# A four-layer attention network on one core: a looser test ahead of layer 0, a new hand-over at the ends of its attention blocks, and layer 1's norms off GpSimd

## The chip, the cores and the metric

The kernel runs on one core of a Trainium2 chip. TensorE (PE) multiplies matrices into PSUM, VectorE (DVE), ScalarE (ACT) and GpSimd (POOL) work element by element, and SyncE (SP) and ScalarE issue DMA transfers. Each engine takes its instructions in the order in which they were written to its own queue, and waits on semaphores for the others. The metric is the device time of one launch in microseconds (us): 5060.61 us before, the median of three runs (5054.19 to 5061.7). All data are float32.

## The reference, cut to what matters

The input x has shape (2, 64, 64, 128): two images of 4096 tokens with 128 channels. Four layers follow one another, each added to x. The change touches the first two:

```
# layer 0: x = x + conv_attention(group_norm(x))
qkv    = xn @ w_qkv                          # 128 -> 3 x 128, 4 heads of 32
scores = q @ k.T * 32**-0.5 + pos            # pos: relative position tables, by row and by column
x      = x + softmax(scores) @ v             # over all 4096 tokens of the image

# layer 1: x = x + triangle(group_norm(x))
xn  = layer_norm(group_norm(x))
l,r = gated projections of xn                # products with sigmoid gates
out = einsum('bkjd,bkid->bijd', l, r) / 64
x   = x + (layer_norm(out) * gate) @ Wo + bo
```

Layers 2 and 3 are attention with a mixture of experts each; nothing of them is changed.

## The kernel before

`layers` runs the four layers in sequence. x stays in SBUF as 64 tiles of 128 tokens.

**The test ahead of layer 0** (`layer0`). A softmax may leave out the subtraction of the row maximum if no score can become too large, and then exponentials of scores and of position terms can be multiplied as separate factors. The kernel tests this on the data. For each image it transposes x in eight groups of 512 tokens (`group_block`, L110 on PE, statistics L113 on VectorE, copy L115 on ScalarE), makes the group norm's mean and root from them (`group_stats`), normalises the transposed image in one VectorE instruction (L289), and then, for each group and for queries and keys, projects 512 tokens (L296), squares the result on ScalarE (L304) and sums the squares of each head by four products with a 128x4 matrix of ones (L306). `tops` takes the maxima. The flag is compared with a limit on VectorE (L244), and every engine loads it and branches: to `l0_bounded`, which is the path taken with these inputs, or to the exact `l0_any`.

**Layer 0's attention** (`l0_bounded`). Eight units (image, pair of heads, half of the queries) of four blocks of 512 queries. A block goes through 32 steps k, one for each 128 keys: a score product into PSUM (L538, four 64x64-tiled matmuls for two heads), the exponential on ScalarE (L546), the multiplication by the exponentials of the column positions on VectorE (L547), and, two steps later, the value product, which adds up in the PSUM tile l0o over the whole block (`values`, L494). l0o holds two partial sums, from the first and the second 64 keys of each step, in its two banks; there is one such tile. At the end of a block its two partial sums are added for each head into the SBUF tile l0os: ScalarE copies the first (L504), VectorE adds the second (L505). `l0_finish` then transposes l0os, divides by the row sums and adds to x. Such follow-up work, and the preparation of the next unit (`l0_prepare`), is cut into pieces that are placed between the steps, one after every second step. The first image's layer-1 norms are among these pieces.

**Layer 1's start** (`layer1`, `l1_rows`). For the second image nothing of layer 0 is left to hide behind. The group norm in token order is a subtraction and a multiplication (`group_norm`, L156 and L157) for each of eight groups of 512 columns, six on VectorE and two on GpSimd; then token statistics on VectorE (L164, L165), a reciprocal root (`rstd`, L93 to L102), the normalisation on VectorE (L168) and ScalarE (L379), transposes (L394) and the gate product (L847), before the projections begin (L875). The addition of the bias bo to x, 16 operations (L924), runs on GpSimd.

The order of the instructions on each queue is fixed when the program is built; a scheduler places the instructions of concurrent strands.

Of the kernel before, what the change touches and what calls it, by code (L numbers as in the profile page):

```python
# [8 lines left out]
F32 = mybir.dt.float32  # L9
AF = mybir.ActivationFunctionType  # L10
# [29 lines left out]
class Net:  # L40
# [111 lines left out]
    def group_norm(self, eng, y, b, g, gb):  # L152

        n0 = b * NC + 4 * g
        row = [gb[:, i * C : (i + 1) * C].unsqueeze(1).broadcast_to([P, 4, C]) for i in range(2)]
        eng.tensor_tensor(y, self.x[:, n0 : n0 + 4, :], row[0], ALU.subtract)  # L156
        eng.tensor_tensor(y, y, row[1], ALU.mult)  # L157
# [95 lines left out]
    def layer0(self, xT, gst, na, nb):  # L253
# [3 lines left out]
        with ExitStack() as st:  # L257
            wp = st.enter_context(tc.tile_pool(reuse_waits="tile", name="l0w", bufs=1))
            w = self.load(wp, "wqkv", [P, 3 * C], ins["L0_conv_w_qkv"])

            pe = wp.tile([P, 2, 2 * S - 1], F32, tag="pe", name="l0pe")
            with (
# [5 lines left out]
                for i, n in enumerate("hw"):  # L268
                    nc.sync.dma_start(out=raw[: 2 * S - 1, i, :], in_=ins[f"L0_conv_pos_emb_{n}"])
# [8 lines left out]

                head = ap.tile([P, NH], F32, tag="head", name="l0head")
                nc.vector.tensor_reduce(  # L280
                    head, self.ident.rearrange("p (h d) -> p h d", d=HD), AX.X, ALU.add
                )

                norms = ps.tile([P, 2, B * NC, NH], F32, tag="norms", name="l0norms", bufs=1)
                for b in range(B):
                    for g in range(NC // 4):
                        self.group_block(ps, gst[:, b], b, g, xT[:, b, :])
                    gm, gr = self.group_stats(ps, gst[:, b], b)
                    nc.vector.tensor_scalar(  # L289
                        xT[:, b, :], xT[:, b, :], gm, gr, ALU.subtract, ALU.mult  # L290
                    )
                    for g in range(NC // 4):
                        cols = slice(g * 512, (g + 1) * 512)
                        for j in range(2):
                            pq = ps.tile([P, 512], F32, tag="misc", name=f"l0n{b}_{g}_{j}")
                            nc.tensor.matmul(  # L296
                                pq,
                                lhsT=w[:, j * C : (j + 1) * C],
                                rhs=xT[:, b, cols],
                                start=True,  # L300
                                stop=True,
                            )
                            sq = ap.tile([P, 512], F32, tag="sq", name=f"l0sq{b}_{g}_{j}")
                            nc.scalar.activation(sq, pq, AF.Square)  # L304
                            for i in range(4):
                                nc.tensor.matmul(  # L306
                                    norms[:, j, b * NC + 4 * g + i, :],
                                    lhsT=sq[:, i * P : (i + 1) * P],
                                    rhs=head,
                                    start=True,  # L310
                                    stop=True,
                                )


                top = self.tops(
                    ps,
                    "l0",
                    [
                        norms[:, 0, :, :].rearrange("p n h -> p (n h)"),
                        norms[:, 1, :, :].rearrange("p n h -> p (n h)"),  # L320
                        posn[:, 0:1],
                        posn[:, 1:2],
                    ],
                )
                s1 = self.small.tile([1, 1], F32, tag="bs1", name="l0s1")
                nc.vector.tensor_tensor(s1, top[:, 2:3], top[:, 3:4], ALU.add)
                nc.vector.tensor_scalar(s1, s1, 4.0, None, ALU.mult)
                s2 = self.small.tile([1, 1], F32, tag="bs2", name="l0s2")
                nc.vector.tensor_scalar(s2, top[:, 1:2], 2.0 / HD, None, ALU.mult)
                nc.vector.tensor_tensor(s1, s1, s2, ALU.add)  # L330
                nc.vector.tensor_tensor(s1, s1, top[:, 0:1], ALU.mult)
                small = self.at_most("l0", s1, 60.0**2)
# [24 lines left out]
    def l1_rows(self, ps, xT, b, st, gb, gpsimd=()):  # L357
# [7 lines left out]
        for g in range(NC // 4):  # L365
            blk = slice(4 * g, 4 * g + 4)
            self.group_norm(nc.gpsimd if g in gpsimd else nc.vector, y[:, blk, :], b, g, gb)
            yield
# [46 lines left out]
    def l0_bounded(self, xT, w, pe, gst, na, nb):  # L415
# [15 lines left out]
        with (  # L431
# [28 lines left out]
            os = wp.tile([P, 512], F32, tag="os", name="l0os")  # L460
# [25 lines left out]
            def values():  # L486
                unit, qb, k, es, o = waiting.pop(0)
# [13 lines left out]
                if k == NC - 1:  # L501
                    for h in range(2):
                        rows = slice(64 * h, 64 * h + HD + 1)
                        nc.scalar.copy(os[rows], o[rows, 0, :])  # L504
                        nc.vector.tensor_tensor(os[rows], o[rows, 1, :], os[rows], ALU.add)  # L505
# [15 lines left out]
            for i, unit in enumerate(units):  # L521
# [6 lines left out]
                for qb in range(4):  # L528
                    qs = slice(qb * 512, (qb + 1) * 512)
                    t = f"{b}_{pair}_{half}_{qb}"  # L530
                    o = None
                    for k in range(NC):
# [17 lines left out]
                        if o is None:  # L550
                            o = ps.tile([P, 2, 512], F32, tag="o", name=f"l0o{t}", bufs=1)
                        waiting.append((unit, qb, k, es, o))
# [98 lines left out]
    def l0_finish(self, ap, ps, unit, qb, os):  # L651
# [4 lines left out]
        yield  # L656
        po = ps.tile([P, 4, 2, 64], F32, tag="misc", name=f"l0po{t}")
        for i in range(4):
            nc.tensor.transpose(
                po[:, i, :, :].rearrange("p h d -> p (h d)"),  # L660
                os[:, i * P : (i + 1) * P],
# [129 lines left out]
    def layer1(self, xT, gst, na, nb, xp, kp):  # L791
# [5 lines left out]
        with ExitStack() as st:  # L797
# [44 lines left out]
            with tc.tile_pool(reuse_waits="tile", name="l1p", bufs=6, space=PSUM) as ps:  # L842
# [11 lines left out]
                rows = self.l1_rows(ps, xT[:, 1, :], 1, gst[:, 1], gb, gpsimd=(6, 7))  # L854
# [44 lines left out]
            with (  # L899
# [4 lines left out]
                for d8 in range(C // 8):  # L904
# [19 lines left out]
                    nc.gpsimd.tensor_tensor(  # L924
# [1236 lines left out]
```

## Time and profile before

| stretch (us) | what | PE busy | clock |
|---|---|---|---|
| 0 to 20 | x is loaded (4 MB) | 0.37 us | - |
| 20.5 to 160 | the test ahead of layer 0 | nearly all of it | 0.50 in most |
| 161 to 206 | preparing the first unit of layer 0 | 0.5 to 0.9 of it | 0.50 to 0.88 |
| 206 to 2320 | layer 0's attention | 2032.7 of 2114 us | 0.99 |
| 2320 to 2385 | layer 1's norms of the second image | 12.9, 1.6 and 10.6 of 20 us each to 2380 | 0.67, 0.50, 0.84 |
| after | rest of layer 1, layers 2 and 3 | - | mostly 1.00 |

PE is busy when a matmul is in it, whatever the clock; "clock" is the share of full speed that the throttle granted. In the listings that follow, a line of the timeline gives the start and the length in us, engine, source line, operation, output and input, the number of instructions merged, and in brackets how long the engine had been idle before and what ended the idleness. A group's line gives the number of instructions, their busy time in us with the mean in ns, and the idle time of the engine just before them with what ended most of it.

### The profile page before, as it was taken

The numbers are of one execution on the slowest core, as the hardware profiler recorded it, in microseconds if no ns is written. First come the engines' busy times: TensorE is split into PE (matmuls) and PEld (weight loads), VectorE is DVE, ScalarE is ACT, GpSimd is POOL, SyncE is SP. The second block draws the span as 40 slices with busy tenths as digits, with TensorE's granted clock in tenths as the row PEclk, the third lists the DMA queues.
The fourth block names the chain that finished last, engine by engine and source line by source line (L and its number), as shares of the span: only waits on it lengthen the run. The fifth ranks groups of instructions, "written<-read, shape, count | busy, mean of one in ns | idle before, by whom it ended". The sixth has DMA issues, their size and how long they took to land.

```text
span 5051.3 us, 79049 instructions
## 1 busy us (share of the span) xinstructions
PE 4668.8 (92%) x33638; PEld 1858.9 (37%) x33638; DVE 2942.8 (58%) x4829; ACT 2696.5 (53%) x3158; POOL 943.6 (19%) x850
## 2 busy tenths in 40 slices
PE   7999999999899999996779999999986999999999
PEld 5533333333333333333522223222334444444443
DVE  1366676767676667776665666555553544454447
ACT  2465555555555555555566766767650433333335
POOL 0100000000000000003445555555540000000008
PEclk6799999999999999998898999999997999999999
DMA  1000000000000000000000000000007000000001
GB/s 36 9 10 1 10 1 10 1 10 1 10 1 10 1 11 1 1 2 7 22 1 1 1 1 1 1 1 1 1 12 258 5 1 0 0 1 0 1 0 35
DMA packets 43359, 60.35 MB, mean 12 GB/s; under 512 B 4497, under 2 KB 25201, under 8 KB 41841
## 3 DMA queue, kind: packets, MB, share of 16 engines
q1 hardware_dynamic: 42096, 54.57, 3.5%
q8 instruction: 268, 4.39, 0.4%
q14 instruction: 99, 0.80, 0.1%
q10 hardware_dynamic: 896, 0.59, 0.0%
HBM read 42.57 MB, written 4.19 MB: 9 GB/s over the span
## 4 chain that ended last, share of the span: by engine, by line
PE 38%; DVE 5%; ACT 3%; POOL 2%; DMA 1%; issue 1%; SPq 0%; DVEq 0%; POOLq 0%; ACTq 0%
PE scl L1998 9%; PE oTl L1958 9%; PE l2sc L1372 5%; PE l2pos L1130 5%; PE l2av L1418 3%; PE f3ex L2092 2%; DVE l2es L1392 2%; POOL l2es L1395 2%; ACT l2es L1403 1%; DMA f2w<-in_L_ffn_weight_dram 1%; ACT l2es L1383 1%; PE l2po L1338 1%; DVE l2a L168 0%; PE l2pu L1130 0%; PE f3fpb L1888 0%
## 5 line engine op out<-in xcount | busy, mean ns | idle before, releaser
L547 DVE TENSOR_TENSOR l0es<-l0es,l0ew 128x1024 f32<-128x1024 f32 x1024 | 1254.6, 1229 | 619.4 <-ACT l0es L546 619.2
L546 ACT ACTIVATE l0es<-l0sc 128x1024 f32<-128x1024 f32 x1024 | 1042.2, 1023 | 701.3 <-PE l0sc L538 699.1
L494 PE MATMUL l0o<-l0es,l0v 64*33 64x512 f32 x8192 | 1093.5, 592 | 65.2 <-DVE l0os L505 59.9
L538 PE MATMUL l0sc<-l0qa,ka 64*64 64x512 f32 x8192 | 1108.9, 596 | 6.6 <-ACT l0es L546 6.6
L1403 ACT ACTIVATE l2es<-l2es 128x1024 f32<-128x1024 f32 (+3 forms) x576 | 559.5, 984 | 271.5 <-POOL l2es L1395 263.6
L1395 POOL TENSOR_TENSOR l2es<-l2es 128x1024 f32<-128x1024 f32 (+3 forms) x352 | 580.9, 1660 | 489.6 <-DVE l2es L1392 433.1
L1966 DVE TENSOR_TENSOR accl<-accl,esl 128x1024 f32<-128x1024 f32 x240 | 293.8, 1224 | 430.4 <-ACT esl L2009 426.5
L1392 DVE TENSOR_SCALAR l2es<-l2sc 128x1024 f32<-128x1024 f32 (+3 forms) x320 | 338.8, 1059 | 316.0 <-PE l2sc L1372 314.8
L494 PEld LDWEIGHTS l0o<-l0es,l0v 64*33 64x33 f32 x8192 | 263.3, 108 | 691.6 <-issue 578.9
L538 PEld LDWEIGHTS l0sc<-l0qa,ka 64*64 64x64 f32 x8192 | 301.9, 133 | 548.4 <-issue 469.7
L2009 ACT ACTIVATE esl<-scl 128x1024 f32<-128x1024 f32 x240 | 245.6, 1023 | 472.9 <-PE scl L1998 446.9
L1998 PE MATMUL scl<-l3qT,l3kT 128*128 128x512 f32 x1024 | 486.3, 595 | 0.0
L1372 PE MATMUL l2sc<-l2q,kept 32*128 32x512 f32 (+3 forms) x2304 | 390.4, 625 | 83.4 <-ACT l2es L1383 63.9
L1958 PE MATMUL oTl<-esl,l3v 128*128 128x512 f32 x960 | 451.0, 592 | 0.0
L672 POOL TENSOR_TENSOR x<-x,l0y 128x256 f32<-128x256 f32 x32 | 23.3, 728 | 2115.3 <-DVE l0y L667 1990.0
L1418 PE MATMUL l2av<-l2es,kept 128*32 128x512 f32 (+3 forms) x2304 | 315.2, 595 | 0.0
L1130 PE MATMUL l2pos<-kept 128*32 128x512 f32 x2416 | 296.9, 599 | 0.0
L1958 PEld LDWEIGHTS oTl<-esl,l3v 128*128 128x128 f32 x960 | 182.1, 190 | 225.4 <-issue 222.1
L1998 PEld LDWEIGHTS scl<-l3qT,l3kT 128*128 128x128 f32 x1024 | 187.2, 191 | 199.6 <-issue 185.7
L1383 ACT ACTIVATE l2es<-l2sc 128x1024 f32<-128x1024 f32 x224 | 226.2, 1010 | 49.7 <-PE l2sc L1372 48.6
L1372 PEld LDWEIGHTS l2sc<-l2q,kept 32*128 32x128 f32 x2304 | 116.7, 188 | 327.0 <-ACT l2es L1383 164.5
L1929 POOL TENSOR_TENSOR bothl<-accl 128x512 f32<-128x512 f32 x16 | 20.2, 1264 | 799.2 <-DVE accl L1966 799.2
(712 smaller groups left out, 4101.2 us busy)
## 6 DMA issues: line engine op xcount, KB each, us to landing
f2w<-in_L_ffn_weight_dram SPq DMA_DIRECT2D x32, 1024.0 KB, 13.1
l0ew<-l0ew SPq DMA_DIRECT2D x16, 512.0 KB, 5.2
x<-in_x_dram SPq DMA_DIRECT2D x8, 512.0 KB, 7.3
out_dram<-x SPq DMA_DIRECT2D x16, 256.0 KB, 2.3
kept<-in_L_attn_pos_rev_dram SPq DMA_DIRECT2D x1, 1792.0 KB
ew<-in_L_ffn_expert_w_dram SPq DMA_DIRECT2D x1, 512.0 KB, 4.2
kept<-in_L_attn_pos_rev_dram SPq DMA_DIRECT2D x1, 256.0 KB, 3.0
f2b<-in_L_ffn_weight_dram ACTq DMA_DIRECT2D x2, 128.0 KB, 2.8
```

The lines of the kernel that those rows point to most:

```text
L494: nc.tensor.matmul(o[64 * h : 64 * h + HD + 1, r, :], lhsT=v1[rows, k, 2 * pair + h, :], rhs=es[rows, h, :], start=(k == 0), stop=(k == NC ...
L538: nc.tensor.matmul(sc[64 * c : 64 * c + 64, h, :], lhsT=ka[rows, k0 : k0 + 64], rhs=qa[rows, k // (NC // 2), qs], start=True, stop=True,)
L546: nc.scalar.activation(es, sc, AF.Exp)
L547: nc.vector.tensor_tensor(es, es, ew[:, :, qs], ALU.mult)
L1130: nc.tensor.matmul(out[part], lhsT=lhsT[:, part], rhs=rhs, start=start, stop=stop)
L1372: nc.tensor.matmul(sc[:, h2, off:], lhsT=kT[hs, k * P : (k + 1) * P], rhs=q[hs, off:], start=True, stop=True,)
L1392: nc.vector.tensor_scalar(es[:, :, lo:], sc[:, :, lo:], root, None, ALU.mult)
L1395: nc.gpsimd.tensor_tensor(part, part, part, ALU.mult)
L1403: nc.scalar.activation(es[:, :, off:], es[:, :, off:], AF.Silu)
L1418: nc.tensor.matmul(avs[i][hs, off:], lhsT=v[:, k, hs], rhs=es[h // 2][:, h % 2, off:], start=(k == 0), stop=last,)
L1958: nc.tensor.matmul(oT, lhsT=vs[b][:, k, :], rhs=es[:, i, :], start=(k == 0), stop=(k == NC - 1),)
L1998: nc.tensor.matmul(sc[:, i, :], lhsT=kTs[b][:, k * P : (k + 1) * P], rhs=qT[:, qb * 512 : (qb + 1) * 512], start=True, stop=True,)
```

## The change

It has three parts, and two small ones that follow from them.

1. The test uses a bound that needs no projection of the tokens. From the weights alone come Gram matrices of each head; traces of their products bound how far a query or a key can be longer than its token, and how large their product can be. What the tokens add is only the largest squared length of a normalised token: each half of an image is normalised by itself, squared (the first half on ScalarE, the second on GpSimd), summed over channels by four products with 32 columns of ones, and its maximum taken. The limit is the same, written without the square (60 in place of 60 squared). The weights and position tables are loaded on ScalarE's queue.
2. At the end of a block, ScalarE copies the first bank of l0o and VectorE the second, for both heads at once, into two halves of l0os; the addition is a piece of `l0_finish`. l0o is one tile for the whole layer and is cleared once.
3. In layer 1, the group norm's last two groups and the bias additions go from GpSimd to VectorE.

Layer 0 now runs before the pool of layer 3's weights is opened, which leaves it more room in SBUF; those small loads move behind layer 0 on SyncE's queue.

```diff
-            w = self.load(wp, "wqkv", [P, 3 * C], ins["L0_conv_w_qkv"])
+            w = wp.tile([P, 3 * C], F32, tag="wqkv", name="wqkv")
+            nc.scalar.dma_start(out=w, in_=ins["L0_conv_w_qkv"])
...
-                    nc.sync.dma_start(out=raw[: 2 * S - 1, i, :], in_=ins[f"L0_conv_pos_emb_{n}"])
+                    nc.scalar.dma_start(
+                        out=raw[: 2 * S - 1, i, :], in_=ins[f"L0_conv_pos_emb_{n}"]
+                    )
...
+                pg = ps.tile([P, 512], F32, tag="misc", name="l0gram")
+                for j in range(2):
+                    wj = w[:, j * C : (j + 1) * C]
+                    nc.tensor.matmul(
+                        pg[:, j * C : (j + 1) * C], lhsT=wj, rhs=wj, start=True, stop=True
+                    )
...
-                    nc.vector.tensor_scalar(
-                        xT[:, b, :], xT[:, b, :], gm, gr, ALU.subtract, ALU.mult
-                    )
-                    for g in range(NC // 4):
-                        cols = slice(g * 512, (g + 1) * 512)
-                        for j in range(2):
-                            pq = ps.tile([P, 512], F32, tag="misc", name=f"l0n{b}_{g}_{j}")
+                    for half in range(2):
+                        part = xT[:, b, half * 2048 : (half + 1) * 2048]
+                        nc.vector.tensor_scalar(part, part, gm, gr, ALU.subtract, ALU.mult)
+                        sq = ap.tile([P, 2048], F32, tag="sq", name=f"l0sq{b}_{half}")
+                        if half:
+                            nc.gpsimd.tensor_tensor(sq, part, part, ALU.mult)
+                        else:
+                            nc.scalar.activation(sq, part, AF.Square)
+                        pn = ps.tile([P, 512], F32, tag="misc", name=f"l0n{b}_{half}")
+                        for i in range(4):
                             nc.tensor.matmul(
-                                pq,
-                                lhsT=w[:, j * C : (j + 1) * C],
-                                rhs=xT[:, b, cols],
+                                pn[HD * i : HD * (i + 1), :],
+                                lhsT=ones,
+                                rhs=sq[:, i * 512 : (i + 1) * 512],
                                 start=True,
                                 stop=True,
                             )
-                            sq = ap.tile([P, 512], F32, tag="sq", name=f"l0sq{b}_{g}_{j}")
-                            nc.scalar.activation(sq, pq, AF.Square)
-                            for i in range(4):
-                                nc.tensor.matmul(
-                                    norms[:, j, b * NC + 4 * g + i, :],
-                                    lhsT=sq[:, i * P : (i + 1) * P],
-                                    rhs=head,
...
+                        nc.vector.tensor_reduce(
+                            most[:, 2 * b + half : 2 * b + half + 1], pn, AX.X, ALU.max
+                        )
...
                 if k == NC - 1:
-                    for h in range(2):
-                        rows = slice(64 * h, 64 * h + HD + 1)
-                        nc.scalar.copy(os[rows], o[rows, 0, :])
-                        nc.vector.tensor_tensor(os[rows], o[rows, 1, :], os[rows], ALU.add)
+                    rows = slice(0, 64 + HD + 1)
+                    nc.scalar.copy(os[rows, 0, :], o[rows, 0, :])
+                    nc.vector.tensor_copy(os[rows, 1, :], o[rows, 1, :])
                     side.insert(0, self.l0_finish(ap, ps, unit, qb, os))
...
         yield
+        nc.vector.tensor_tensor(os[:, 0, :], os[:, 0, :], os[:, 1, :], ALU.add)
+        yield
         po = ps.tile([P, 4, 2, 64], F32, tag="misc", name=f"l0po{t}")
...
-                rows = self.l1_rows(ps, xT[:, 1, :], 1, gst[:, 1], gb, gpsimd=(6, 7))
+                rows = self.l1_rows(ps, xT[:, 1, :], 1, gst[:, 1], gb)
...
-                    nc.gpsimd.tensor_tensor(
+                    nc.vector.tensor_tensor(
                         xs, xs, bo.unsqueeze(1).broadcast_to([P, 4, C]), ALU.add
                     )
```

## The prediction

> **What bounds the kernel now.** I read the shares of the page first:
>
> ```profile
> PE 4668.8 (92%) x33638; PEld 1858.9 (37%) x33638; DVE 2942.8 (58%) x4829; ACT 2696.5 (53%) x3158; POOL 943.6 (19%) x850
> PEclk6799999999999999998898999999997999999999
> ```
>
> TensorE is busy 92% of the span, so the kernel as a whole is TensorE's; what a part of the change gives is the TensorE time or idleness it takes away in its own stage. The second line is the granted clock in slices of 126 us: 0.6 in the first, where the change begins. The page's chain of waits goes back only into the second layer (its shares add up to about half of the span), so the first 2400 us are read from stretches and the timeline.
>
> Stage A, the test before layer 0 (0 to 161 us). The windows (columns: stretch, length, busy PE, PEld, DVE, ACT, POOL, clock, DMA share, GB/s) and the groups between 30 and 161 us:
>
> ```profile
> 60.00:80.00 20.00, 20.00 (x61) 14.04 (x60) 0.00 (x0) 3.58 (x6) 0.00 (x0) 0.50 0.00 0
> ...
> L296 PE MATMUL l0n<-xT,wqkv 128*128 128x512 f32 x64 | 65.0, 1127 | 7.9 <-DVE xT L289 4.0 <-issue 3.9
> L306 PEld LDWEIGHTS l0norms<-l0head,l0sq 128*128 128x128 f32 x256 | 62.1, 334 | 31.1 <-issue 30.0 <-ACT l0sq L304 1.1
> ```
>
> TensorE is alone at work, at half clock, with VectorE idle. In the timeline a 512-column block of one projection costs 3.41 us (L296 starts at 49.04, 52.46, 55.87), and there are 32: 16 per image. They fill 33.7 to 87.9 and 101.6 to 156.4 us. The flag is computed at 160.23 and layer 0 proper begins at 161.2.
>
> Stage B, the attention loop (206 to 2320 us): PE is busy 2032.7 of 2114 us at clock 0.99. Of its 81 us of idleness the groups put 59.9 down to one wait, "L494 PE MATMUL l0o <-DVE l0os L505", 30 times: the end of each 512-query block. One of them in the timeline:
>
> ```profile
> 352.92 0.68 DVE L505 TENSOR_TENSOR l0os<-l0o,l0os 33x512 f32<-33x512 f32 x1
> 353.63 0.58 ACT L504 COPY l0os<-l0o 33x512 f32<-33x512 f32 x1 [1.42 <-DVE l0os L505]
> 354.24 1.02 ACT L546 ACTIVATE l0es<-l0sc 128x1024 f32<-128x1024 f32 x1
> 354.25 0.69 DVE L505 TENSOR_TENSOR l0os<-l0o,l0os 33x512 f32<-33x512 f32 x1 [0.65 <-ACT l0os L504]
> 355.00 1.49 PE L494 MATMUL l0o<-l0es,l0v 64*33 64x512 f32 x11 [1.77 <-DVE l0os L505]
> ```
>
> Copy, add, copy, add run one after another, although the two heads touch different rows; PE stands 1.77 us until the last add has read l0o (2.45 where other pieces delay it).
>
> Stage C, layer 1's start (2312 to 2385 us): VectorE is the path, and PE is busy 1.64 of 20 us in 2340 to 2360. The same operation beside GpSimd, and alone inside layer 0's loop:
>
> ```profile
> L156 DVE TENSOR_TENSOR xT<-x,l1gb 128x512 f32<-128x512 f32 x6 | 10.3, 1755 | 0.0
> ...
> L156 DVE TENSOR_TENSOR xT<-x,wqkv x8: 682/684/693, 1335.6 to 1349.3; 128x512 f32<-128x512 f32 x8
> ```
>
> **What the Trainium skill says.** "SBUF — State Buffer", section "Who interferes with whom": a VectorE instruction with two SBUF inputs takes its second one through the read interface it shares with GpSimd. The trace agrees: 1755 against 684 ns. "TensorE: Matmul & The Clock Gate", Part 1: the clock is half by default and sustained activity releases it. Here it stayed at 0.50 with PE busy 20.00 of 20 us, so for these 4-column products the measurement decides; but after the 2.45 us stall that ended at 1072.19 the clock did fall to 0.50 for some 3 us, which fits. "DMA: Bandwidth & Descriptors", section "Queues, rings and completion order": SyncE's and ScalarE's transfers have rings of their own, served in turn by packet. No trace of before shows two queues competing.
>
> **The change, part by part.**
>
> *A, the test.* It removes all 32 steps. Instead: loads of weights and position tables on ScalarE's queue; a short chain on the weights; per image two norms of 2048 columns, a square on ScalarE and one on GpSimd, and for each half four products with 32 columns of ones. The built order has the second image's transposes behind the first image's last product on PE, and both maxima ahead of its statistics on VectorE, so the two images stay in series. The sum:
> - Position tables land: before, issued at 15.09 behind x, PE saw them at 19.18. On their own ring, first in the queue, like the first x transfer (4.5 us to landing): taken 6 us. Ends: 4 and 20 us (behind all of x).
> - Weight chain ahead of the first transpose on PE: gram, mask, product, copy, product, sum, traces. Eight or nine short steps of 0.28 to 0.5 us: 4.2. First transpose at 10.2 us; x of image 0 is there about 11.5 (fourth transfer, issued near 4, plus 7.3), before its last blocks are due.
> - First transpose to normalised start: 20.48 to 31.18 before, 10.7 us. Now 20.9.
> - Two half norms: 2.41 us as before: 23.3.
> - GpSimd's square of 128x2048 is no row. Its in-place squares (L1395) are 613, 1040, 1466 and 1893 ns for 256 to 1024 columns: 1.67 ns each, so 3.6 us. "GPSIMD Engine Reference", section 3.1, has 4.5 for a two-input operation of this size; that is the upper end. ScalarE's half (about 2 us from L897's 1066 ns for 1024) is hidden beside it. 26.9.
> - Four 32-column products at half clock: 0.85 us each in L296, 3.4 in series; 0.85 if they share the array like L538's four (0.86 for four 64-column tiles, full clock). Taken 2.0: 28.9.
> - Image 1 again, 10.7 + 2.4 + 3.6 + 2.0: 47.6. Maximum 0.7, then ten small steps (before: about 0.18 each after the maxima) 2.4: flag at 50.7.
> The flag was written by 160.4, so A gives 110 less a margin: **109 us** (91 with the late tables and slow ends, 114 with the early ones). After the flag the same work follows; VectorE's new memset of l0o and longer one of l0os (about 1.6 us more) end before its first copy at 166.1 in the old clock, which waits for ScalarE.
>
> *B, block ends.* One ScalarE copy (97 rows), one VectorE copy, and the add moved off the bank. In the built order the VectorE copy waits for ScalarE's; that costs nothing, since ScalarE's copy ends at 352.21 and VectorE is free only at 352.92, behind the two products L547 queued ahead. From there the copy takes 0.69 (L585, 128x512 from PSUM) plus 0.07 to release: PE resumes at 353.7 instead of 355.0. 1.32 us, 30 times: 39.6. The last end of the loop has the three in series, 1.95 against 2.63: 0.7. Behind the new add (0.68, SBUF) stands the next L547, needed by PE only after two more value and score groups, some 3.4 us later: hidden. The extra piece per block: 4 of 16 slots instead of 3, and there are free ones. **40 us.** If the copy sat behind another piece it would be half: 20.
>
> *C, clock.* The windows at 800 to 820 and 1060 to 1080 have 0.91, each after a 2.45 us stall: 20 x 0.09 = 1.8 us lost, twice. With stalls of 1.1 us: **3.6 us**. The stretch 1340 to 1400 (0.90, 0.84, 0.91) is another queue's; not counted, 7 us at most.
>
> *D, layer 1.* VectorE's 12 operations of 1.75 us (20.9; 20.1 by the timeline) become 16 of 0.684 (10.9): 9.2 less. But 10 of the 16 bias adds moved to VectorE stand, in the built order, between the statistics and the steps of the reciprocal root, which before took 3.4 us there: 10 x 0.684 + 1.4 = 8.2, 4.8 more. The other six fall where VectorE idled 26 us before L883: nothing. SyncE issues five small loads (0.43 us each) later, ahead of the gate weights: 1 us at most. **3.4 us** less, between -3 and 9.
>
> Sum: 109 + 40 + 3.6 + 3.4 = 156; 5060.6 - 156 = **4905 us**.
>
> **Rivals.**
> 1. *The loads land behind x, and the squares are slow* (A = 91): 18 less, 4923. For: 290 GB/s were in flight from 4 to 16 us. Against: separate rings.
> 2. *Block ends: the wait moves to VectorE's queue* (B = 20): 4925. For: VectorE's two L547 stand ahead of the copy. Against: they end at 352.9 already.
> 3. *More comes back*: all the clock loss, and products in parallel (7 + 5 more): 4893 or a little lower.
> 4. *Slower: the looser bound sends layer 0 into the exact branch.* That is 2048 steps of one score product (0.43) and eight 128-column ones (0.12 each, 64 of L403 in 7.59 us): 2.8 ms of PE against 2.1, about 5650 us. Against: worked out from the inputs, the longest token's square is 207.4 and the bound 15.7 + 31.4 = 47.1, under the limit of 60. Also here: some unforeseen jam.
>
> **How the numbers follow.** Forecast 0.68, rival 1 0.12, rival 2 0.08, rival 3 0.10, rival 4 0.02. The range takes in 1 to 3 with a little over, 4882 to 4935. Faster 0.98, same 0.005, slower 0.015.
>
> **What would show it.** A: the first L538-like score product near 90 us instead of 197, and no PE group of 60 us before it. B: the wait of the value product for l0os near 0.45 us each, some 14 us in all. C: no 0.91 windows after block ends. D: layer 1's 128x512 subtract and multiply at 684 ns, and the first l1p product about 3 us nearer to the loop's end. Wrong: a flag later than 70 us, PE waits of over 1 us at block ends, or a score product that is 128 queries wide.

## The result, and the profile after

The changed kernel takes 4906.38 us (median of four runs, 4900.87 to 4914.85) against 5058.49 (four runs, 5054.19 to 5061.7): a ratio of 0.9701, 95% interval 0.9684 to 0.9718, or 152 us less; predicted were 4905 us and 156 less. In the runs of the experiments the kernel before shows two levels, 5000 to 5008 us in 12 of 29 runs and 5053 to 5067 in the others, so the intervals against it are wide there and the experiments are compared among themselves, by their medians and traces; the eighth of them bears on what lies behind the two levels.

The trace after is of the slowest of its four runs (span 4913.0 us). A second trace of the same program, taken later (the last run below, span 4897.1), stands beside it, because single traces of one program differ in places:

| part | predicted gain | first trace | second trace |
|---|---|---|---|
| start to first score product (A) | 109 | 197.23 - 97.31 = 99.9 | 197.23 - 96.06 = 101.2 |
| first score product to the loop's last addition (B and C) | 43.6 | 2114.9 - 2072.4 = 42.5 | 2114.9 - 2068.0 = 46.9 |
| from there to the first projection of layer 1 (D) | 3.4 | 72.56 - 72.14 = 0.4 | 72.56 - 66.42 = 6.1 |
| the rest | 0 | 2666.6 - 2671.2 = -4.6 | 2666.6 - 2666.6 = 0 |
| sum (spans) | 156 | 138.2 | 154.2 |

The 4.6 us lost in the rest of the first trace were not followed further; the second trace, of the same program, doesn't have them.

Shares and clock of the page after:

```profile
PE 4556.6 (93%) x33360; PEld 1785.9 (36%) x33360; DVE 2937.1 (60%) x4864; ACT 2666.8 (54%) x3100; POOL 922.1 (19%) x832
PEclk7999999999999999988899999999978999999999
```

PE's busy time fell by 112.2 us, 100.9 of them ahead of the flag (125.5 to 24.6 us in the windows). The share hardly moves (92 to 93%): a share can't show a gain of 3%, the stages can.

**The test**, in the timeline (start, length, engine, line; in brackets the idle time before and what ended it):

```profile
1.94 3.15 ACTq L271 DMA_DIRECT2D l0raw<-in_L_conv_pos_emb_w_dram  x1
...
8.86 0.37 PE L275 MATMUL l0peh<-ident,l0raw 128*32 128x128 f32 x1 [8.86 <-DMA l0raw<-in_L_conv_pos_emb_h_dram]
13.15 0.40 PE L275 MATMUL l0pew<-ident,l0raw 128*32 128x128 f32 x1 [3.92 <-DMA l0raw<-in_L_conv_pos_emb_w_dram]
...
18.39 5.91 PE L110 MATMUL gt<-ident,x 128*128 128x128 f32 x32
...
29.24 2.60 DVE L353 TENSOR_SCALAR xT<-xT,gm,gr 128x2048 f32<-128x2048 f32 x2
...
58.51 0.14 DVE L245 TENSOR_SCALAR bok_l<-l0s 1x1 int32<-1x1 f32 x1
```

The flag comes at 58.5 us; 160.2 before. Up to the first transpose the stage is late: the second position table is used at 13.15 us, predicted was 6. From there on it keeps to the prediction: 10.85 us to the normalised image (10.7 predicted).

**A block's end** in the timeline after, the counterpart of the five lines in the prediction:

```profile
249.91 0.58 ACT L555 COPY l0os<-l0o 97x512 f32<-97x512 f32 x1
250.04 1.23 DVE L597 TENSOR_TENSOR l0es<-l0es,l0ew 128x1024 f32<-128x1024 f32 x1 [0.46 <-ACT l0es L596]
...
251.19 0.68 DVE L556 COPY l0os<-l0o 97x512 f32<-97x512 f32 x1
251.91 0.69 DVE L705 TENSOR_TENSOR l0os<-l0os 128x512 f32<-128x512 f32 x1
...
251.93 1.06 PE L546 MATMUL l0o<-l0es,l0v 64*33 64x512 f32 x8 [1.29 <-DVE l0os L556]
```

ScalarE's copy has ended at 250.49. VectorE's doesn't run beside it: it starts at 251.19, when the 1.23-us product ahead of it in VectorE's queue ends, and PE resumes when it ends. The group of the value products over the loop (busy, mean ns, idle before and by whom):

```profile
L546 PE MATMUL l0o<-l0es,l0v 64*33 64x512 f32 x8192 | 1069.8, 592 | 51.7 <-DVE l0os L556 46.4 <-DVE l0es L597 5.0
```

PE still waits 46.4 us for the buffer, not 14; before it was 59.9. Yet a block without extra pieces takes 57.19 us (from 251.93 to 309.12) against 58.53 (355.00 to 413.53), 1.34 less; 1.32 were predicted. TensorE's order resolves this. Its rows in the trace before, ahead of the wait that ended at 355.00, and in the trace after:

```profile
350.48 1.04 PE L494 MATMUL l0o<-l0es,l0v 64*33 64x512 f32 x8
351.34 1.89 PE L538 MATMUL l0sc<-l0qa,ka 64*64 64x512 f32 x14
```

```profile
248.74 1.04 PE L546 MATMUL l0o<-l0es,l0v 64*33 64x512 f32 x8
249.60 1.04 PE L588 MATMUL l0sc<-l0qa,ka 64*64 64x512 f32 x8
```

Before, PE worked another 1.89 us ahead of the wait, nearly two score products; after, 1.04. A score product of 0.86 us has gone from before the wait to behind it, so PE arrives that much earlier and waits that much longer: 1.77 - 1.34 + 0.86 = 1.29, which is the wait in the trace.

**Layer 1's norms** by group, after; then the gate products behind them, in the first and in the second trace:

```profile
L157 DVE TENSOR_TENSOR xT<-x,l1gb 128x512 f32<-128x512 f32 x8 | 5.1, 684 | 0.0
L158 DVE TENSOR_TENSOR xT<-xT,l1gb 128x512 f32<-128x512 f32 x8 | 5.1, 682 | 0.0
```

```profile
L897 PE MATMUL l1pg<-xT,wcat 128*128 128x512 f32 x16 | 14.7, 1016 | 11.1 <-ACT xT L444 11.1
```

```profile
L897 PE MATMUL l1pg<-xT,wcat 128*128 128x512 f32 x16 | 10.0, 707 | 12.9 <-ACT xT L444 12.9
```

The norms are at 684 ns as predicted. The same 16 gate products take 1016 ns in one trace and 707 in the other: in the first, six of eight passes ran at half clock (2.07 us per pair), in the second one. That stretch is 33.0 us long in the first and 27.9 in the second; in the kernel before it is 27.9 too, with one pass at half clock.

### The profile page after: what moved, and what is told of

Read it like the earlier page. It is cut to its first block, busy times and chain, and to the rows that moved or that the text cites. A ratio compares the mean times of both kernels' runs of the same rounds, so it can differ in the third digit from the quotient of the medians.

```text
span 4913.0 us, 78463 instructions
## 1 busy us (share of the span) xinstructions
PE 4556.6 (93%) x33360; PEld 1785.9 (36%) x33360; DVE 2937.1 (60%) x4864; ACT 2666.8 (54%) x3100; POOL 922.1 (19%) x832
## 4 chain that ended last, share of the span: by engine, by line
PE 38%; DVE 6%; ACT 3%; POOL 3%; issue 2%; DMA 0%; POOLq 0%; DVEq 0%; ACTq 0%
PE scl L2048 9%; PE oTl L2008 9%; PE l2sc L1422 5%; PE l2pos L1180 4%; PE l2av L1468 3%; PE f3ex L2142 2%; DVE l2es L1442 2%; POOL l2es L1445 2%; ACT l2es L1453 1%; ACT l2es L1433 1%; PE l2po L1388 1%; DVE l2a L169 0%; PE f3fpb L1938 0%; PE l2pu L1180 0%; PE f2pp L1613 0%
## 5 line engine op out<-in xcount | busy, mean ns | idle before, releaser
L546 PE MATMUL l0o<-l0es,l0v 64*33 64x512 f32 x8192 | 1069.8, 592 | 51.7 <-DVE l0os L556 46.4
L588 PE MATMUL l0sc<-l0qa,ka 64*64 64x512 f32 x8192 | 1081.9, 597 | 4.7 <-ACT l0es L596 4.6
```

The costliest lines, as they stand in the source:

```text
L546: nc.tensor.matmul(o[64 * h : 64 * h + HD + 1, r, :], lhsT=v1[rows, k, 2 * pair + h, :], rhs=es[rows, h, :], start=(k == 0), stop=(k == NC ...
L588: nc.tensor.matmul(sc[64 * c : 64 * c + 64, h, :], lhsT=ka[rows, k0 : k0 + 64], rhs=qa[rows, k // (NC // 2), qs], start=True, stop=True,)
```

## The experiments

Ten experiments ran. Medians in us; "flag" is the start of the comparison; the loop is from the first score product to the last addition; the wait is PE's for l0os, summed over the ends.

| kernel | time | flag | first score | loop | wait |
|---|---|---|---|---|---|
| before | 5058.5 | 160.23 | 197.23 | 2114.9 | 59.9 |
| changed | 4906.4 | 58.51 | 97.31 | 2072.4 | 46.4 |
| e1, test only | 4952.6 | 58.73 | 97.52 | 2114.3 | 59.5 |
| e2, block ends only | 4987.2 | 159.72 | 196.81 | 2070.4 | 46.4 |
| e3, layer 1 only | 5049.6 | 159.87 | 196.86 | 2115.0 | 59.9 |
| e4, tables first | 4895.5 | 51.15 | 88.48 | 2067.9 | 46.4 |
| e5, freed copies | 4899.8 | 58.84 | 97.69 | 2064.5 | 16.1 |
| e6, copy first | 4861.9 | 58.99 | 97.80 | 2028.4 | 3.4 |
| e7, all | 4851.9 | 47.42 | 84.88 | 2030.3 | 3.6 |
| e8, before with a warm start | 5010.3 | 113.28 | 150.70 | 2114.0 | 59.5 |
| e9, all and kept warm | 4850.3 | 45.78 | 82.30 | 2028.2 | 3.4 |
| e10, changed again | 4902.8 | 58.80 | 96.06 | 2068.0 | 46.4 |

**The parts, each alone on the kernel before.** e1 has the new test (and the pools in the order of the change), e2 the block ends, e3 layer 1.

```diff
 # e1: part 1 of the diff alone
-                norms = ps.tile([P, 2, B * NC, NH], F32, tag="norms", ...)
+                        sq = ap.tile([P, 2048], F32, tag="sq", name=f"l0sq{b}_{half}")
 # e2: part 2 alone
-                        nc.vector.tensor_tensor(os[rows], o[rows, 1, :], os[rows], ALU.add)
+                    nc.vector.tensor_copy(os[rows, 1, :], o[rows, 1, :])
 # e3: part 3 alone
-                    nc.gpsimd.tensor_tensor(
+                    nc.vector.tensor_tensor(
                         xs, xs, bo.unsqueeze(1).broadcast_to([P, 4, C]), ALU.add
```

> The kernel before with the new test alone; block ends and layer 1 as before. Theory: the parts add up, and the test's gain is the 100 us by which the changed kernel's first score product came earlier (97.3 against 197.2 us, of which 101.7 at the flag and 1.8 given back behind it). About 4958 us, first score product at 96 to 97 us (the 1.8 us belong to the memsets of the block ends' buffers, which are not in this kernel, so 1 to 2 us may be missing here), loop as long as before (2115 us), PE's waits at the block ends 1.77 us each as before. Rival: part of the 100 us was paid back by a cooler clock or by collisions later in the loop; then the loop is longer than 2115 us by several us and the time is over 4965.

Measured: 4952.63 us (4944.06 to 4958.02), ratio 0.9806 (0.9741 to 0.9871). The first score product comes 99.7 us earlier, the loop is as long as before and so are its waits: the test's gain arrives whole, and nothing of it is paid back later. One detail of the expectation fell: from the flag to the first score product it takes 38.8 us here without the larger memsets, 37.1 in e2 with them and 37.3 in the second trace of the changed kernel. So the memsets do not cost the 1.8 us; in two traces of one program this stretch differs by 1.5.

> The kernel before with the block ends of the change alone. Theory 1 (what the changed kernel's trace says): each block's period falls by 1.32 us though TensorE still waits 1.29 us there, because its order at the end differs as well: one score product (0.86 us) that used to run ahead of the wait now runs behind it. Then the loop is 2072 us against 2115, the time about 5016, and the sum of the waits for the copied buffer about 46 us. Theory 2 (as predicted): with the old test in front the wait is near 0.45 us each, 14 us in all, and the loop is also about 43 us shorter. The time doesn't tell these apart, the sum of the waits does. Rival: the gain in the loop came from the earlier start and not from the ends; then the time is near 5058.

Measured: 4987.22 us (4953.13 to 5011.45; two of the four near 5010, two near 4960), ratio 0.9852 (0.977 to 0.9933). The loop alone, in the trace, is 44.5 us shorter. PE's wait, by group:

```profile
L497 PE MATMUL l0o<-l0es,l0v 64*33 64x512 f32 x8192 | 1067.7, 591 | 52.1 <-DVE l0os L507 46.4 <-DVE l0es L548 5.5
```

46.4 us again, with the old test in front: theory 1. The wait that stays comes with the block ends themselves.

> The kernel before with layer 1's norms and bias additions on VectorE alone, nothing else changed. Theory (as predicted): from the end of layer 0's last addition to the first transpose of the normalised rows 44.7 us before falls by 4 to 5.5 us, and to the first left-right projection 72.6 us falls by 3.4; about 5055 us, within the scatter of the timing. Rival 1: the stretch behind those transposes runs at half clock for most of its 28 us (0.56 on average there in the changed kernel against 0.83 before), because TensorE has been idle in front of it, and takes 33 instead of 28: then the first projection comes no earlier than before and the time is 5058 or over. Rival 2: the half clock there is chance; then this run may show the 28 us.

Measured: 5049.61 us (4989.57 to 5057.15, twelve runs), ratio 0.9984 (0.9936 to 1.0032): inconclusive as it stands, because both kernels have runs on both levels. Taken level by level it is 7 to 11 us faster: medians of 5050.3 (nine runs) against 5057.6 (ten) on the upper level, and 4990.4 (three) against 5001.1 (five) on the lower. One trace tells the steps: from the last addition to the first transpose of normalised rows 39.0 us against 44.7, so 5.7 gained. It consists of 10.4 for the norms (9.7 us against 20.1), less 1.6 for the later start of the norms, less 3.1 for the bias additions (15.5 against 12.4 us from the norms' end). Five of the eight passes behind it ran at half clock, and of the 5.7 us 1.8 are left at the first projection in this trace. That is rival 1 in its size, but rival 2 in its cause: of the other traces, e2, whose layer 1 is as before, has seven such passes, and the second trace of the changed kernel has one.

**Tables first.** The changed kernel with the three small loads on SyncE's queue ahead of x.

```diff
-            nc.scalar.dma_start(out=w, in_=ins["L0_conv_w_qkv"])
 ...
+                nc.sync.dma_start(out=w, in_=ins["L0_conv_w_qkv"])
+                for g in range(0, B * NC, 8):
+                    nc.sync.dma_start(out=self.x[:, g : g + 8, :], in_=src[:, g : g + 8, :])
```

> The changed kernel with the position tables and the layer's weights on SyncE's queue ahead of x, instead of on ScalarE's queue beside x; nothing else. Theory: the tables' landing at 8.9 and 13.2 us is what put the first transpose at 18.4 instead of the 10.2 us of the prediction; alone in front they land by 6 us, the chain on the weights (5.0 us) ends near 11, the transposes of the first image start there if x has landed, and the flag comes 5 to 7 us earlier (51.5 to 53.5 instead of 58.5): about 4900 us. Rival: x, issued three loads later, becomes the last to land; its fourth block was needed 11 us after the start before, so the transposes then stall on x and the flag comes only 2 to 3 us earlier. Second rival: the queue isn't the reason for the late landing (the first load of a queue is slow anyway); then the tables land at 9 to 13 again and nothing is gained.

Measured: 4895.49 us (4890.5 to 4900.75), ratio 0.9693 (0.963 to 0.9757). In the timeline:

```profile
4.38 0.37 PE L279 MATMUL l0peh<-ident,l0raw 128*32 128x128 f32 x1 [4.38 <-DMA l0raw<-in_L_conv_pos_emb_h_dram]
5.47 0.39 PE L279 MATMUL l0pew<-ident,l0raw 128*32 128x128 f32 x1 [0.72 <-DMA l0raw<-in_L_conv_pos_emb_w_dram]
...
10.72 4.08 PE L107 MATMUL gt<-ident,x 128*128 128x128 f32 x24
...
51.15 0.14 DVE L242 TENSOR_SCALAR bok_l<-l0s 1x1 int32<-1x1 f32 x1
```

The tables are used 7.7 us earlier, the first transpose comes 7.7 earlier and the flag 7.4 earlier. The landing was nearly the whole of the missing gain. With the landing that the prediction had assumed, its flag at 50.7 us is met to about half a microsecond. Nothing waited for x, though it was issued three loads later.

**Block ends, what binds them.** e5 puts the two banks of l0o, and the halves of l0os, into tiles of their own; e6 moreover has VectorE's copy ahead of the step's product, by writing the product behind the value products in every step.

```diff
 # e5
-            o = ps.tile([P, 2, 512], F32, tag="o", name="l0o", bufs=1)
+            o = [ps.tile([P, 512], F32, tag=f"o{i}", name=f"l0o{i}", bufs=1) for i in range(2)]
 # e6, in addition
-                        nc.vector.tensor_tensor(es, es, ew[:, :, qs], ALU.mult)
                         if len(waiting) == 2:
                             values()
+                        m = nc.vector.tensor_tensor(es, es, ew[:, :, qs], ALU.mult)
+                        if k == 1:
+                            tc.keep_in_program_order(m)
```

> The changed kernel with the two halves of l0o, and of l0os, made into tiles of their own, so that VectorE's copy at a block end waits for TensorE alone and no longer for ScalarE's copy; in VectorE's queue it still stands behind the 1.23-us product of that step. Theory (VectorE's queue is the bound: in the changed kernel's trace the copy starts the moment that product ends, 0.7 us after ScalarE's copy has ended): nothing changes, period 57.19 us, PE's wait 1.29 us each, time within 2 us of 4906. Rival (the copies bind one another): the copy starts with ScalarE's, PE resumes 0.7 us sooner at 30 ends, 20 us less, about 4886.

Measured: 4899.81 us (4898.47 to 4905.86), ratio 0.9733 (0.9672 to 0.9795). VectorE's copy in the timeline, and the group of the value products:

```profile
248.98 1.22 DVE L599 TENSOR_TENSOR l0es<-l0es,l0ew 128x1024 f32<-128x1024 f32 x1 [0.47 <-ACT l0es L598]
...
250.12 0.68 DVE L557 COPY l0os<-l0o 97x512 f32<-97x512 f32 x1
```

```profile
L548 PE MATMUL l0o<-l0es,l0v 64*33 64x512 f32 x8192 | 1157.4, 590 | 21.8 <-DVE l0os L557 14.3 <-DVE l0es L599 5.5 <-ACT l0os L558 1.8
```

The copy stands behind the product as before, and the period is still 57.2 us (the additions start at 250.91 and 308.10). The time is 3 us below the second median of the changed kernel, within what two medians of one program differ. What changed is the wait: 16.1 us instead of 46.4 (14.3 for VectorE, 1.8 for ScalarE), because PE now runs two value products ahead of VectorE's copy (from 249.47 us), and its busy time rises by 87.6 us in this group alone: behind the copy its records show value and score products in turn, mostly one to four at a time, where eight of a kind stood together, so the records of the two kinds overlap. A wait of 30 us vanished, and the time it took did not.

> As the kernel with the freed copies, and VectorE's copy now stands ahead of the product of that step in VectorE's queue. Theory (that product is the bound): the copy starts when the last value product ends, some 0.2 us before the product would have started, ends 1.25 us sooner than in the changed kernel, and PE hardly waits: its wait at the ends falls from 1.29 to under 0.2 us each, the sum from 46 to under 10 us, the period from 57.19 to 55.9; 30 times about 1.25 is 37 us, about 4868. Rival: the delayed product (0.7 us later) makes TensorE wait for l0es behind it, and part comes back: a new wait for l0es of up to 0.7 us per end, 4890.

Measured: 4861.92 us (4861.28 to 4867.26), ratio 0.9658 (0.9597 to 0.9719). The same end in the timeline, and the group:

```profile
247.53 0.69 DVE L557 COPY l0os<-l0o 97x512 f32<-97x512 f32 x1 [0.29 <-PE l0o L548]
247.57 0.58 ACT L558 COPY l0os<-l0o 97x512 f32<-97x512 f32 x1
248.14 1.22 DVE L601 TENSOR_TENSOR l0es<-l0es,l0ew 128x1024 f32<-128x1024 f32 x1
248.20 1.14 PE L548 MATMUL l0o<-l0es,l0v 64*33 64x512 f32 x8
```

```profile
L548 PE MATMUL l0o<-l0es,l0v 64*33 64x512 f32 x8192 | 1090.6, 591 | 9.1 <-DVE l0es L601 5.5 <-ACT l0os L558 1.8 <-DVE l0os L557 1.6
```

Now the two copies are side by side, PE goes on without a wait, the period is 55.87 us (55.9 expected) and the loop 40 us shorter than in the second trace of the changed kernel; the time is 38 us below e5's. No new wait for l0es appears: 5.5 us as in e5. The product ahead of the copy was the bound.

**Everything together.** e7 joins e4 and e6, and TensorE takes the second image's transposes ahead of the first image's products of ones:

```diff
+                blocks(0)
+                sq0 = squares(0)
+                blocks(1)
+                maxima(0, sq0)
+                sq1 = squares(1)
+                maxima(1, sq1)
```

> Everything that the runs so far suggest, together: the changed kernel with tables first on SyncE's queue (flag at 51.3 instead of 58.5 us), the copy first at block ends, and the second image's transposes ahead of the first image's products of ones in TensorE's order, so that the two images of the test overlap. Theory: the second image's normalised start comes 5 us sooner (its transposes run under the first image's two normalisations, 5.2 us, and its square), flag near 46 us; with 37 us from the ends the sum is 4906 - 7 - 5 - 37 = 4857. Rival: the statistics of the second image and the normalisation of the first meet on VectorE, which then is the path, and the overlap gives 2 us or nothing: flag at 49 to 51, 4862.

Measured: 4851.86 us (4847.58 to 4858.18), ratio 0.9637 (0.9575 to 0.9698): faster than both kernels, 51 to 55 us below the two medians of the changed one. The flag comes at 47.42 us, 3.7 before e4's, between theory (46) and rival (49 to 51). The second image's norm starts at 36.25 us. VectorE took three of its statistics only behind the first image's norms: the rival's collision, costing part of the gain.

**A warm start for the old test.** The kernel before, with dense products on TensorE while x is loaded:

```diff
+                warm = ps.tile([P, 512], F32, tag="misc", name="warm")
+                for i in range(28):
+                    nc.tensor.matmul(
+                        warm, lhsT=self.ident,
+                        rhs=self.ident.unsqueeze(1).broadcast_to([P, 4, P]), start=True, stop=True)
```

> The kernel before with 28 dense products of 512 columns (their result unused) on TensorE from 1.4 us on, where it otherwise idles until 19 us; nothing else. In the last runs the kernels with the old test fell into two groups 55 us apart (5055 to 5067 and 5000 to 5008 for the kernel before), those with the new test did not; every profile so far shows the longer one, with the old test at clock 0.50. Theory 1: the half clock of the old test is what makes the longer group, and it holds because TensorE enters that stage cold; entered warm, the 16 steps of an image run at nearly full clock, the flag comes at about 105 us instead of 160, and the time is about 5003. Theory 2: products of 4 columns can't hold the clock whatever came before; then the clock falls to 0.50 soon after the first of these steps, the flag stays at 155 to 165, and the time is 5055 with the same two groups.

Measured: 5010.29 us (5007.57 to 5018.24), ratio 0.9953 (0.989 to 1.0016); none of the four runs is on the upper level. Two stretches of the test (columns as in the prediction), and two of its products:

```profile
40.00:60.00 20.00, 20.00 (x108) 13.83 (x107) 0.00 (x0) 6.77 (x12) 0.00 (x0) 0.95 0.00 0
80.00:100.00 20.00, 20.00 (x103) 13.64 (x103) 0.00 (x0) 6.57 (x11) 0.00 (x0) 0.93 0.01 1
```

```profile
44.58 1.10 PE L305 MATMUL l0n<-xT,wqkv 128*128 128x512 f32 x2
45.52 0.95 PE L315 MATMUL l0norms<-l0head,l0sq 128*128 128x4 f32 x8
```

Theory 1 holds in its first half: with the clock at 0.93 to 0.95 in these stretches, the same instructions take 1.10 and 0.95 us where they took 2.06 and 1.71 all through the stage before. From the first transpose to the flag it is 86.1 us instead of 139.8, 53.6 less. The flag came at 113.3 us and not at 105; the warming products, which ended 27.1 us after the start, cost 6.7 of that. The two levels of the kernel before lie 54 us apart, and only kernels with the old test had them. The mean clock of the runs agrees: 0.945 to 0.949 on the upper level, 0.957 to 0.960 on the lower, and 0.956 to 0.959 in e8. That the lower level is this same stage at full clock is thus likely, but no trace of an unwarmed run on that level was taken.

Its second half, that the half clock holds because TensorE enters the stage cold, is not shown. These are the first products of an image, in the trace before and here, and the clock around them here:

```profile
33.69 3.75 PE L296 MATMUL l0n<-xT,wqkv 128*128 128x512 f32 x4 [3.95 <-issue]
```

```profile
38.66 3.52 PE L305 MATMUL l0n<-xT,wqkv 128*128 128x512 f32 x4 [3.95 <-issue]
```

```profile
36.00:38.00 2.00, 0.00 (x0) 0.00 (x0) 1.96 (x2) 0.00 (x0) 0.00 (x0) 0.50 0.00 0
40.00:42.00 2.00, 2.00 (x3) 0.64 (x2) 0.00 (x0) 0.60 (x1) 0.00 (x0) 0.54 0.00 0
42.00:44.00 2.00, 2.00 (x14) 1.50 (x13) 0.00 (x0) 0.60 (x1) 0.00 (x0) 1.00 0.00 0
```

Both stages begin after 3.95 us of idle TensorE and at half clock: by 36 us the clock was back at 0.50. In e8 the clock then rose at 41.8 us, some 3 us after these products began, and at 82.8 us, some 3 us after those of the second image (79.64). In the trace before it did not rise after either. Besides, 12 of 29 runs of the kernel before reached the lower level without any warming, so four of four could be chance, if not a likely one (17 of 49 runs of kernels with the old test; to the fourth power about 1 in 70, an estimate).

A reading that fits, but was not tested: every stretch of one clock in e8's trace is a multiple of 3.41 us (6.83, 34.13, 6.83 and 27.31 from 35.0 us on), as if the clock were set anew in steps of that length. In the traces of before, e2 and e3 the first products of each image began 1.6 to 2.1 us into such a step, and the clock stayed down; in e8 both began 0.3 us into one and nearly filled it, and it rose at its end. By this reading what counts is where in a step the four dense products fall.

**Kept warm.** e7 with six dense products behind the second image's statistics and six behind the last maximum:

```diff
                 sq1 = squares(1)
+                warm(6, "a")
                 maxima(1, sq1)
                 top = self.tops(ps, "l0", [most])
+                warm(6, "b")
```

> The kernel with all improvements so far, and twelve dense products of 512 columns (results unused) in TensorE's gaps near the end of the test: six behind the second image's statistics, six behind the last maximum. Theory (from the warm start: what TensorE did just before sets the clock of the next stretch): the stretch from the flag to the first score product, 37.5 us long at a granted clock of 0.57 to 0.65, then runs nearly at full clock and is some 8 to 10 us shorter, while the flag comes at most 3 us later because the dense products stand ahead of the real ones; about 4846 against 4852. Rival: the gap at the branch on the flag cools the clock again, nothing is gained, and the delay stays: 4853 to 4856.

Measured: 4850.26 us (4847.83 to 4852.39), ratio 0.9638 (0.955 to 0.9725), not to be told from e7. From the flag to the first score product it takes 36.5 us instead of 37.5, with the clock from 48 to 90 us at 0.72 against 0.64. The flag came 1.6 us earlier, not later. The expected 8 to 10 us did not come: a miss, and not the rival's either, because the clock holds at the branch. It is 1.00 from 40 us on and falls at about 58.6 us, under work:

```profile
54.98 4.03 PE L678 MATMUL l0pw<-l0qa,l0pe 32*64 32x32 f32 x128 [0.68 <-ACT l0qa L669]
59.24 7.04 PE L678 MATMUL l0pw<-l0qa,l0pe 32*64 32x32 f32 x128 [0.24 <-ACT l0ew L690]
```

```profile
55.00:60.00 5.00, 4.76 (x142) 4.63 (x144) 0.65 (x1) 4.09 (x4) 4.96 (x3) 0.86 0.01 3
60.00:65.00 5.00, 5.00 (x98) 5.00 (x98) 0.00 (x0) 3.32 (x4) 1.91 (x2) 0.50 0.02 3
```

The second 128 of these products of 32 columns take 7.04 us where the first took 4.03, with TensorE busy all the while. Small products kept it busy here, but not at full clock; waits of 2 us come only later. The clock is back at about 82.5 us, behind four products of 512 columns (from 78.62).

**The changed kernel again.**

> The changed kernel as it is, on the same chip as the last version, for a comparison with it and for a second look at the two places where single traces differ. Expected: 4900 to 4915 us with no group 55 us apart, since the old test is gone; flag at 58.5 us; of the eight passes in front of the first left-right projection a number between one and seven at half clock (33 us for that stretch with six, 27.9 with one), which would show that this is chance and not the change's; loop 2065 to 2073 us.

Measured: 4902.8 us (4898.96 to 4909.33), ratio 0.9745 (0.9656 to 0.9833; four of the seven runs of before beside it were on the lower level). One of eight passes at half clock, 27.9 us, so the six of the first trace come and go from run to run of one program. By this trace layer 1's part gains 6.1 us.

## Why the prediction was right, step by step

The time was right (4905 predicted, 4906.4 measured), and so were the large steps; three terms were mis-sized (2, 5 and 6), and the half clock of the old test was taken as given (3). That the sum was met to 1.4 us is in part luck: A gave 8 us too little, while in the second trace B and C gave 3.3 and D 2.7 too much.

1. *Test, duration.* Right. First transpose to norm 10.85 us (10.7), the two half norms 2.60 (2.4), GpSimd's square 3.60 (3.6), the four products 1.94 (2.0), the flag's tail 2.1 (2.4). e1 shows that the gain arrives whole.
2. *Test, landing of the tables.* Wrong: "taken 6 us", measured 13.15, within the bounds kept (4 to 20); rival 1's first half came true in part: late, but not behind all of x. "DMA: Bandwidth & Descriptors", section "Queues, rings and completion order", of the Trainium skill says that rings are served in turn by packet; a ring of one's own did not give an early landing here, beside x at 223 GB/s. e4 shows that order in one queue did. The weight chain took 5.0 us instead of 4.2. Together 8 us: A was 101.7 at the flag instead of 109.
3. *Test, clock.* The prediction took the half clock of the old test as given, and said that for 4-column products "the measurement decides". e8 shows that the same products can run at 0.93 to 0.95. "TensorE: Matmul & The Clock Gate", Part 1, has sustained activity release the clock; e8 agrees, its clock rising some 3 us after the first products of each image, while the trace before shows that the stage can also stay at 0.50 with PE busy 20.00 of 20 us. What decides between the two stays open. Of A's 100 us some 54 are, by e8, half clock. Against a run of before on its lower level, near 5003, the change gives about 100 us, not 152.
4. *Block ends, gain.* Right: 1.34 us per end (1.32 predicted), 57.19 against 58.53. The prediction had it that VectorE's copy is bound by the products queued ahead of it, and e5 and e6 confirm that.
5. *Block ends, the wait.* Wrong: "near 0.45 us each, some 14 us in all", measured 1.29 and 46.4. It took PE's wait before, less the gain, for the wait after, which holds only if PE arrives at the wait at the same time. The new order has one score product less ahead of it. The listed counter-sign ("PE waits of over 1 us at block ends") therefore appeared though the step was right.
6. *Clock after block ends.* Not as predicted: windows at 0.91 remain, at 940 and 1760 us, where the wait is 2.03 us. The value product behind the first of them, with its group before and after:

```profile
951.36 1.93 PE L546 MATMUL l0o<-l0es,l0v 64*33 64x512 f32 x8 [2.03 <-DVE l0os L556]
953.07 1.88 PE L588 MATMUL l0sc<-l0qa,ka 64*64 64x512 f32 x8
954.77 1.03 PE L546 MATMUL l0o<-l0es,l0v 64*33 64x512 f32 x8
```

   The stall is shorter than 2.45 us but still followed by two groups at half clock. The 3.6 us are not found as such; four loops of this program's block ends measure 2067.9 to 2072.4, a gain of 42.5 to 47 for B and C together, against 43.6.
7. *Layer 1.* Right in kind and near in size: 5.7 us to the first transpose (e3), of which the norms gave 10.4 (9.2 predicted) and the bias additions took 3.1 (4.8). What of it reaches the first projection, 0.4 to 6.1 us in three traces, went with the clock of the next 30 us: six, five and one of eight passes at half clock left 0.4, 1.8 and 6.1 us.

## What to carry to other kernels

An engine's idle time at a wait is no sure measure of what removing the wait will give: it moves with what that engine's own queue holds ahead of the wait and behind it, as 59.9, 46.4 and 16.1 us at the same hand-over did, while the time followed only the end of the last reader. So look for what stands ahead of that reader in its own queue; here one product, moved behind the copy, was worth 40 us more than the second copy alone. And when a stage runs at half clock, find out whether it must, before its length is taken as the price of its instructions.

## What the runs showed of the hardware

A busy TensorE did not always have the full clock. One sequence of 512-column products and 4-column products, with TensorE busy 20.00 of 20 us, stayed at 0.50 through both images in the trace before and, once released, ran at 1.00 in e8, though it began at 0.50 in both. In e9 the clock fell from 1.00 to 0.50 under products of 32 columns, and stayed there with TensorE busy 5.00 of 5 us. After a stall of 2.03 us it fell too, for two groups. The passes ahead of layer 1's projections, identical in all kernels, had between one and seven of eight at half clock, 27.9 to 34.3 us. And a small load on a queue of its own was not early: issued at 1.94 us on ScalarE's queue beside x, with 3.15 us of issuing, the table was used at 13.15; issued at 1.56 ahead of x on the same queue as x, at 5.47.
